# Mixture-of-experts results accumulated in DRAM instead of scattered, read back and added

## The chip, the cores and the metric

The kernel runs on one core of a Trainium2 chip. The metric is the device time of one execution in microseconds (us). All data are float32 unless said otherwise. The core has five engines that run side by side and meet at semaphores: PE (matrix multiply), DVE (vector), ACT (activation functions), POOL (GpSimd, which here also issues the scatters by index), and SP, whose queue issues most plain DMAs.

## The reference, cut to what matters

The whole program is four residual blocks on 4096 tokens of 128 features: a causal convolution with softmax weights, a feed-forward block with FP4-quantized operands, an attention block with two inner training steps, and a mixture of experts. Only the last one matters here:

```python
probs = softmax(layernorm(x) @ Wg + bg)                 # E = 8 experts
gate_vals, exp_idx = top_k(probs, 2)                    # K = 2 experts for a token
gate_vals = gate_vals / sum(gate_vals)
capacity = ceil(1.2 * T * K / E)                        # T = 4096 tokens: 1229 slots an expert
# every expert takes up to 1229 tokens, the rest of its slots stay empty
h  = gelu(buf[e] @ W1[e] + b1[e])                       # 1229 x 128 -> 1229 x 512
ye = h @ W2[e] + b2[e]                                  # 1229 x 512 -> 1229 x 128
out[token] = sum over its two experts of gate * ye[slot of the token]
x = x + out
```

## The kernel before

The tokens live in SBUF as `cx.x`, 128 partitions x 32 tiles x 128 features, in eight groups of four tiles (`G = 4`, `W = 512` columns). Three tables in DRAM belong to the experts (class `Slots`): `rows`, 9856 rows of 130 numbers (a token's normalized features, its result row and its weight; expert e owns `PITCH` = 1232 rows); `res`, 8192 rows of 128 for results, one for each token and choice; and `last`, 4096 rows for the last expert's results, one for each token. `clear` (L1117) fills `rows` with empty entries and `res` and `last` with zeros, by three DMAs on SP's queue, at the end of the first block.

Routing (`route`, from L1198) is called once for each group during the last part of the third block. Each call computes the layernorm, the two experts, the weights and the slots of 512 tokens, and POOL issues eight scatters of 128 rows into `rows` (L1278). The addition that finishes a group's `x` is L876 on DVE.

`experts` (from L1297) then loops over the eight experts. SP loads an expert's slots into `xe` (L1333 for nine full tiles of 128 slots, L1337 for the last 77), two buffers; the loads wait for all routing scatters. A piece is four tiles (512 columns), so an expert is pieces of 4, 4 and 2 tiles. For each piece PE transposes the tiles (`tp`, L1356), DVE copies them (`xt`, L1358), PE multiplies by W1 into four banks `ph` (L1362), ACT applies GELU (`ht`, L1365), PE multiplies by W2 (`po`, L1371), DVE adds the bias (`ye`, L1380) and multiplies by the weight (L1384), and POOL scatters each tile's 128 rows to DRAM (L1386). `ye` has four buffers. Empty slots carry a row number past the table's end, and a bounds check drops them:

```python
1386  sc = nc.gpsimd.indirect_dma_start(
1387      out=(self.slots.last if last else self.slots.res)[:, :],
1388      out_offset=bass.IndirectOffsetOnAxis(ap=num[:m, c0 + i, :], axis=0),
```

For the last expert, DVE first turns the row numbers into token numbers (`tok`, L1345 to L1348). Experts 0 to 6 write to `res`, the last to `last`.

At the end `gather` (L1313) reads `res` back in sixteen DMAs of 256 KB (`y`, L1318, SP's queue, after all scatters to `res`), and DVE adds each to `x` (L1319); then it does the same with `last` in eight DMAs, on SP and ACT. Each finished group goes out by a DMA (L1427, SP's queue).

The order on each engine is fixed at build time from the order of the program and the waits between instructions; an engine executes its list in order. DMAs of one kind share eight semaphores in turn, so a ninth one waits for the first.

Of the kernel before, what the change touches and what calls it, by code (L numbers as in the profile page):

```python
# [8 lines left out]
I32 = mybir.dt.int32  # L9
# [1088 lines left out]
class Slots:  # L1098
# [4 lines left out]
    def __init__(self, cx, stack):  # L1103
        nc, tc = cx.nc, cx.tc
        dram = stack.enter_context(tc.tile_pool(name="d_dram", bufs=1, space=DRAM))
        self.rows = dram.tile([R, DX], F32, tag="rows", name="rows")
        self.res = dram.tile([K * T, D], F32, tag="res", name="res")
        self.last = dram.tile([T, D], F32, tag="last", name="last")
        n = R // P
        m = 7  # L1110
        self.empty = cx.const.tile([P, m, DX], F32, tag="empty", name="empty")
        nc.gpsimd.memset(self.empty, 0.0)
        nc.gpsimd.memset(self.empty[:, :, D : D + 1].bitcast(I32), K * T)
        self.n, self.m = n // m, m

    def clear(self, cx, ins):

        nc = cx.nc
        by_p = self.rows.rearrange("(p a m) d -> p a (m d)", p=P, m=self.m)
        src = flat(self.empty).unsqueeze(1).to_broadcast([P, self.n, self.m * DX])  # L1120
        after(cx.tc, nc.sync.dma_start(out=by_p, in_=src), ins)
        src = cx.const.tile([P, 4 * D], F32, tag="zero", name="zero")
        nc.gpsimd.memset(src, 0.0)
        for t in (self.res, self.last):
            n = t.shape[0] // P // 4
            by_p = t.rearrange("(p a m) d -> p a (m d)", p=P, m=4)
            after(cx.tc, nc.sync.dma_start(out=by_p, in_=src.unsqueeze(1).to_broadcast([P, n, 4 * D])), ins)


class Moe:  # L1130
# [29 lines left out]
    def open_router(self, stack):  # L1160
        cx = self.cx
        nc, tc = cx.nc, cx.tc
        cp = stack.enter_context(tc.tile_pool(name="r_c", bufs=1))
        self.p2 = stack.enter_context(tc.tile_pool(name="r_p2", bufs=2))
        self.ps_t = stack.enter_context(tc.tile_pool(name="r_pst", bufs=1, space=PSUM))
        self.ps_r = stack.enter_context(tc.tile_pool(name="r_psr", bufs=1, space=PSUM))
        tp = self.ps_t.tile([P, E * NF], F32, tag="t", name="tp")
        nc.tensor.transpose(tp, self.b1_rows, cx.ident[: E * NF, : E * NF])
        nc.scalar.copy(self.b1.rearrange("p e c -> p (e c)"), tp)
        self.ones = cp.tile([P, P], F32, tag="ones", name="ones")  # L1170
        nc.gpsimd.memset(self.ones, 1.0)
# [12 lines left out]
        self.rank = cp.tile([P, G, E], F32, tag="rank", name="rank")  # L1184
        nc.gpsimd.iota(
            self.rank, [[0, G], [-1, E]], base=E, channel_multiplier=0, allow_small_or_imprecise_dtypes=True
        )

        self.xr = cp.tile([P, K, NT, DX], F32, tag="xr", name="xr")
        num = cp.tile([P, K, NT], I32, tag="num", name="num")  # L1190
        nc.gpsimd.iota(num, [[T, K], [P, NT]], base=0, channel_multiplier=1)
        nc.gpsimd.tensor_copy(self.xr[:, :, :, D : D + 1].bitcast(I32), num.unsqueeze(3))

        self.seen = cp.tile([P, K, E], F32, tag="seen", name="seen")
        nc.gpsimd.memset(self.seen, 0.0)
        self.limit = nc.gpsimd.to_reg(R - 1)

    def route(self, g):  # L1198
# [8 lines left out]
            return t.unsqueeze(2).to_broadcast([P, G, E])  # L1207

        x, at = grp(cx.x, g), slice(g * G, (g + 1) * G)
        tp = self.ps_t.tile([P, G, P], F32, tag="t", name="tp")  # L1210
        for j in range(G):
            nc.tensor.transpose(tp[:, j, :], x[:, j, :], cx.ident)
# [84 lines left out]
    def experts(self):  # L1297
# [5 lines left out]
        done, ended = [], []  # L1303
        by_t = self.slots.res.rearrange("(k n p) d -> p k n d", k=K, p=P)
        last_t = self.slots.last.rearrange("(n p) d -> p n d", p=P)
        with ExitStack() as st:
            p2 = st.enter_context(tc.tile_pool(name="d_p2", bufs=2))
            ps_t = st.enter_context(tc.tile_pool(name="d_pst", bufs=2, space=PSUM))
            ps_h = st.enter_context(tc.tile_pool(name="d_psh", bufs=4, space=PSUM))
            ps_o = st.enter_context(tc.tile_pool(name="d_pso", bufs=2, space=PSUM))  # L1310
            limit, last_limit = nc.gpsimd.to_reg(K * T - 1), nc.gpsimd.to_reg(T - 1)

            def gather(src, k, names, first, engines):  # L1313

                for g in range(NG):
                    y = p2.tile([P, G, D], F32, tag="y", name="y", bufs=8)
                    eng = engines[g % len(engines)]
                    self.after(eng.dma_start(out=y, in_=src[:, k, g * G : (g + 1) * G, :]), names)  # L1318
                    ad = nc.vector.tensor_tensor(grp(cx.x, g), grp(cx.x, g), y, ALU.add)  # L1319
                    tc.add_manual_dep(  # L1320
                        ad.ins, first.ins.name,
                        mybir.DependencyInfo(mybir.DependencyClass.NoSync, mybir.DependencyReason.DATA),
                        reason="experts first",
                    )

            for e in range(E):
                xe = p2.tile([P, NR, DX], F32, tag="xe", name="xe")
                base = e * PITCH
# [7 lines left out]
                )  # L1336
                self.after(nc.sync.dma_start(out=xe[:left, NR - 1, :], in_=rows[full : base + CAP, :]), every)  # L1337
                num = xe[:, :, D : D + 1].bitcast(I32)
                if last:

                    tok = p2.tile([P, 3, NR], I32, tag="tok", name="tok")
                    for lo, k, m in ((0, NR - 1, P), (NR - 1, 1, left)):
                        t = tok[:m, :, lo : lo + k]
                        n = num[:m, lo : lo + k, 0]
                        nc.vector.tensor_scalar(t[:, 0], n, float(T), None, ALU.is_ge)  # L1345
                        nc.vector.tensor_scalar(t[:, 1], n, float(K * T), None, ALU.is_lt)
                        nc.vector.tensor_tensor(t[:, 0], t[:, 0], t[:, 1], ALU.mult)
                        nc.vector.scalar_tensor_tensor(t[:, 2], t[:, 0], -float(T), n, ALU.mult, ALU.add)  # L1348
                    num = tok[:, 2, :].unsqueeze(2)
                for c0 in range(0, NR, G):  # L1350
                    tiles = range(c0, min(c0 + G, NR))
                    size = [left if i == NR - 1 else P for i in tiles]
                    n = sum(size)
                    tp = ps_t.tile([P, W], F32, tag="t", name="tp")
                    for i, m in zip(tiles, size):
                        nc.tensor.transpose(tp[:, (i - c0) * P : (i - c0) * P + m], xe[:m, i, :D], cx.ident[:m, :m])  # L1356
                    xt = p2.tile([P, W], F32, tag="xt", name="xt")
                    last_in = nc.vector.tensor_copy(xt[:, :n], tp[:, :n])  # L1358
# [17 lines left out]
                    for lo, k, m in ((0, nf, P), (nf, len(size) - nf, left)):  # L1376
# [7 lines left out]
                        last_out = nc.vector.tensor_tensor(y, y, w, ALU.mult)  # L1384
                        for i in range(lo, lo + k):
                            sc = nc.gpsimd.indirect_dma_start(  # L1386
                                out=(self.slots.last if last else self.slots.res)[:, :],
                                out_offset=bass.IndirectOffsetOnAxis(ap=num[:m, c0 + i, :], axis=0),
                                in_=ye[:m, i, :], in_offset=None,
                                bounds_check=last_limit if last else limit, oob_is_err=False,  # L1390
                            )
                            tc.declare_no_dep(sc.ins, group="results", reason="rows of their own")
                            tc.add_to_no_dep_group("results", sc.ins)
                            (ended if last else done).append(sc.ins.name)
            gather(by_t, 0, done, last_in, (nc.sync,))
            gather(by_t, 1, done, last_out, (nc.sync,))
            gather(last_t.unsqueeze(1), 0, ended, last_out, (nc.sync, nc.scalar))


def moe(cx):  # L1400
# [45 lines left out]
```

## Time and profile before

| | |
|---|---|
| Median of three timed runs | 1364.11 us (1363.63 to 1365.26) |
| Profiled execution, its own time | 1367.42 us |
| Its span, first to last instruction | 1365.7 us |
| Mean granted clock of PE | 0.927 |
| Busy: PE, DVE, ACT, POOL | 82%, 57%, 36%, 56% of the span |
| First scatter of results, last one issued | 1180.9 us, 1346.9 us |
| First output DMA issued | 1353.5 us |

The profile is one execution. A row of a group names line, engine and operation, what it writes and reads, the count, the busy time in us and the mean of one in ns, then the idle time of the engine just before such instructions and what ended most of it. "issue" is time in which the engine waited for nothing that the profile shows. A row of the timeline gives start and length in us; a "q" behind an engine's name means its queue, that is DMA issues and waits. The chain of waits lists the work that ended last, in order of time. The PE rows count each of these float32 matrix products as two instructions.

### The profile page before, as it was taken

To read this page: it belongs to the slowest core of one execution; us is meant where nothing else is said; L and a number is where in the kernel's file an instruction comes from. 1 tells how busy PE (TensorE), PEld (TensorE's weight loads), DVE (VectorE), ACT (ScalarE), POOL (GpSimd) and SP (SyncE) were. 2 spreads that over 40 slices of the span, in tenths; PEclk is the share of its full clock that TensorE was granted. 3 is DMA by queue.
4 is the path that set the end of the run, shared out by engine and by line. 5 is a ranking of instruction groups with operands and counts; after the bars stand their busy time and mean duration, and the time that the engine had idled before them with its cause. 6 is when DMAs were issued, how large, how long until landed. Compare 5 with 4: busy or idle time off the path is not lost.

```text
span 1365.7 us, 15325 instructions
## 1 busy us (share of the span) xinstructions
PE 1122.8 (82%) x5211; PEld 661.2 (48%) x5211; DVE 776.2 (57%) x1754; ACT 493.7 (36%) x1002; POOL 761.5 (56%) x724
## 2 busy tenths in 40 slices
PE   4688888726878689999998999999898873799981
PEld 1233333314656445555556455555665442576761
DVE  8689899978796544444445444444556564122233
ACT  4534455325555632222234222222442221333320
POOL 4336566644554588888841888888104336244533
PEclk9888899976999999999999999999999886899996
DMA  4322223924000000000000000000000001222146
GB/s 133 90 73 73 73 73 95 348 82 143 1 0 1 0 0 1 0 0 1 1 1 1 1 0 1 0 1 1 0 1 30 24 28 43 57 60 63 48 114 182
DMA packets 61614, 63.07 MB, mean 46 GB/s; under 512 B 6767, under 2 KB 44478, under 8 KB 61536
## 3 DMA queue, kind: packets, MB, share of 16 engines
q1 hardware_dynamic: 54016, 52.37, 13.1%
q0 software_dynamic: 4608, 8.43, 2.0%
q10 hardware_dynamic: 2912, 1.29, 0.4%
q8 instruction: 41, 0.67, 0.2%
q14 instruction: 37, 0.30, 0.1%
HBM read 37.90 MB, written 25.04 MB: 46 GB/s over the span
## 4 chain that ended last, share of the span: by engine, by line
issue 62%; PE 10%; DMA 2%; DVE 1%; SPq 1%; POOL 1%; POOLq 0%; ACT 0%; another core or an unknown queue 0%; DVEq 0%
PE po L1371 5%; PE ph L1362 5%; DMA w<-in_L_ffn_W 1%; POOL last L1386 1%; DMA y<-last 1%; PE tp L1356 0%; POOLq L1442 0%; DVE ye L1380 0%; DVE xt L1358 0%; DMA xe<-rows 0%; DMA L_ffn_bg<-in_L_ffn_bg 0%; SPq L604 0%; SPq L710 0%; DMA last<-ye,tok 0%; SPq L59 0%
## 5 line engine op out<-in xcount | busy, mean ns | idle before, releaser
L1051 POOL TENSOR_TENSOR ds<-sw,s 128x512 f32<-128x512 f32 x64 | 81.4, 1272 | 86.7 <-DVE sw L1046 86.7
L1278 POOL DMA_INDIRECT rows<-xr,slot x64 | 62.4, 976 | 104.9 <-DVE rs L93 55.6
L1386 POOL DMA_INDIRECT res<-ye,xe x70 | 68.2, 974 | 89.6 <-DVE ye L1384 36.3
L1053 POOL TENSOR_TENSOR ds<-ds,s 128x512 f32<-128x512 f32 x64 | 112.1, 1751 | 5.0
L391 PE MATMUL cv<-pr,sel 128*32 128x512 f32 x512 | 78.4, 691 | 22.5 <-DVE pr L381 22.4
L1044 ACT COPY b<-pb 128x512 f32<-128x512 f32 x64 | 37.4, 585 | 162.1 <-PE pb L1040 161.6
L1365 ACT ACTIVATE ht<-ph,b 128x512 f32<-128x512 f32 (+1 forms) x96 | 55.5, 602 | 107.9 <-PE ph L1362 96.5
L1048 DVE TENSOR_TENSOR h<-sw,b 128x512 f32<-128x512 f32 x64 | 50.2, 784 | 70.6 <-ACT b L1044 70.1
L1371 PEld LDWEIGHTS po<-w,ht 128*128 128x128 f32 (+1 forms) x640 | 79.5, 193 | 15.3 <-issue 9.5
L1052 POOL TENSOR_TENSOR ds<-sw,ds 128x512 f32<-128x512 f32 x64 | 82.5, 1289 | 5.0
L1371 PE MATMUL po<-w,ht 128*128 128x128 f32 (+1 forms) x640 | 83.0, 284 | 2.7 <-ACT ht L1365 2.6
L1054 POOL TENSOR_TENSOR ds<-ds,b 128x512 f32<-128x512 f32 x64 | 81.4, 1271 | 5.0
L1076 PEld LDWEIGHTS pp<-proj,ht 128*128 128x128 f32 x512 | 67.1, 191 | 30.7 <-issue 29.8
L1362 PE MATMUL ph<-xt,w 128*128 128x512 f32 (+1 forms) x192 | 73.9, 522 | 9.6 <-DVE xt L1358 7.6
L383 POOL TENSOR_TENSOR pr<-base,en 128x512 f32<-128x512 f32 x48 | 69.6, 1479 | 21.7 <-ACT en L345 21.7
L381 DVE TENSOR_TENSOR pr<-base,w 128x3072 f32<-128x3072 f32 x24 | 79.6, 3318 | 2.5 <-ACT w L343 2.5
L1380 DVE TENSOR_TENSOR ye<-po,b 128x512 f32<-128x512 f32 (+2 forms) x32 | 14.9, 488 | 112.7 <-PE po L1371 87.1
L1046 DVE TENSOR_TENSOR sw<-pa,s 128x512 f32<-128x512 f32 x64 | 44.2, 691 | 53.6 <-ACT s L1042 53.6
L1071 ACT COPY ht<-pt 128x512 f32<-128x512 f32 x64 | 37.4, 585 | 101.6 <-PE pt L1069 101.6
L1086 PE MATMUL ph<-proj_t,dpt 128*128 128x512 f32 x128 | 71.6, 641 | 0.0
L1088 DVE TENSOR_TENSOR db<-ph,sw 128x512 f32<-128x512 f32 x64 | 44.2, 691 | 47.4 <-PE ph L1086 47.4
L1038 PE MATMUL pa<-gate,kt 128*128 128x512 f32 x128 | 66.8, 604 | 2.5 <-ACT b L1044 2.4
(320 smaller groups left out, 2665.0 us busy)
## 6 DMA issues: line engine op xcount, KB each, us to landing
base<-far SPq DMA_DIRECT2D x64, 268.0 KB
rows<-empty SPq DMA_DIRECT2D x1, 5005.0 KB
xe<-rows SPq DMA_DIRECT2D x8, 585.0 KB
res<-zero SPq DMA_DIRECT2D x1, 4096.0 KB
w<-in_L_ffn_W SPq DMA_DIRECT2D x16, 256.0 KB
y<-res SPq DMA_DIRECT2D x16, 256.0 KB
far<-avg SPq DMA_DIRECT2D x8, 272.0 KB
x<-in_L_attn_x SPq DMA_DIRECT2D x8, 256.0 KB
```

Source lines behind the costliest of these rows:

```text
L381: vec(nc.vector.tensor_tensor(pr[:, :nv, :], s["base"][:, :nv, at], w.to_broadcast([P, nv, L]), ALU.mult))
L383: nc.gpsimd.tensor_tensor(pr[:, d, :], s["base"][:, d, at], s["en"][:, g, :], ALU.mult)
L391: ten(nc.tensor.matmul(s["cv"][32 * j : 32 * (j + 1), :], sel[:, i].rearrange("p a h -> p (a h)"), s["pr"][g][:, i * NJ + j, :], start=(g ...
L1051: nc.gpsimd.tensor_tensor(ds, sw, s, ALU.mult)
L1052: nc.gpsimd.tensor_tensor(ds, sw, ds, ALU.subtract)
L1053: nc.gpsimd.tensor_tensor(ds, ds, s, ALU.add)
L1054: nc.gpsimd.tensor_tensor(ds, ds, b, ALU.mult)
L1076: nc.tensor.matmul(pp, ht[:, c * P : (c + 1) * P], proj[:, c, :], start=(c == 0), stop=(c == NF - 1))
L1086: nc.tensor.matmul(ph, dpt, proj_t, start=True, stop=True)
L1362: nc.tensor.matmul(ph[:, :n], self.w1[:, e, c * P : (c + 1) * P], xt[:, :n], start=True, stop=True)
L1371: nc.tensor.matmul(po[:m, i - c0, :], ht[:, c, at : at + m], self.w2[:, e, c, :], start=(c == 0), stop=(c == NF - 1),)
L1386: sc = nc.gpsimd.indirect_dma_start(out=(self.slots.last if last else self.slots.res)[:, :], out_offset=bass.IndirectOffsetOnAxis(ap=num[: ...
```

## The change

The two result tables go. In their place stands `sums`, 4096 + 1232 rows of 128. While a group is routed, SP copies its finished `x` into `sums`. The experts' scatters add their rows to the token's row in `sums` (an accumulating DMA, issued by POOL). Row numbers are now token numbers for both choices; an empty slot's number is 4096 plus its place in the expert, so that it falls on a row that is not read. DVE computes these numbers in `to`, for each expert. Since a token can belong to two experts, an expert's first scatter waits until the scatters of the expert before have landed: POOL writes a small tile `gate` that waits for them. The last expert's pieces are 4, 2, 2 and 2 tiles. After the last scatters SP writes one row of zeros past the tokens, and the output is copied from `sums` by the eight DMAs, DRAM to DRAM. There is no reading back and no addition on DVE.

```diff
         self.rows = dram.tile([R, DX], F32, tag="rows", name="rows")
-        self.res = dram.tile([K * T, D], F32, tag="res", name="res")
-        self.last = dram.tile([T, D], F32, tag="last", name="last")
+        self.sums = dram.tile([T + PITCH, D], F32, tag="sums", name="sums")
...
-        nc.gpsimd.memset(self.empty[:, :, D : D + 1].bitcast(I32), K * T)
+        nc.gpsimd.memset(self.empty[:, :, D : D + 1].bitcast(I32), T)
...
     def clear(self, cx, ins):
...
-        src = cx.const.tile([P, 4 * D], F32, tag="zero", name="zero")
-        nc.gpsimd.memset(src, 0.0)
-        for t in (self.res, self.last):
-            n = t.shape[0] // P // 4
-            by_p = t.rearrange("(p a m) d -> p a (m d)", p=P, m=4)
-            after(cx.tc, nc.sync.dma_start(out=by_p, in_=src.unsqueeze(1).to_broadcast([P, n, 4 * D])), ins)
...
-        nc.gpsimd.iota(num, [[T, K], [P, NT]], base=0, channel_multiplier=1)
+        nc.gpsimd.iota(num, [[0, K], [P, NT]], base=0, channel_multiplier=1)
...
         x, at = grp(cx.x, g), slice(g * G, (g + 1) * G)
+        nc.sync.dma_start(out=self.slots.sums[:T, :].rearrange("(n p) d -> p n d", p=P)[:, at, :], in_=x)
...
-            def gather(src, k, names, first, engines):
-
-                for g in range(NG):
-                    y = p2.tile([P, G, D], F32, tag="y", name="y", bufs=8)
-                    eng = engines[g % len(engines)]
-                    self.after(eng.dma_start(out=y, in_=src[:, k, g * G : (g + 1) * G, :]), names)
-                    ad = nc.vector.tensor_tensor(grp(cx.x, g), grp(cx.x, g), y, ALU.add)
...
+            place = p2.tile([P, NR], I32, tag="place", name="place", bufs=1)
+            nc.gpsimd.iota(place, [[P, NR]], base=0, channel_multiplier=1)
+            added = []
             for e in range(E):
...
-                if last:
-
-                    tok = p2.tile([P, 3, NR], I32, tag="tok", name="tok")
...
-                for c0 in range(0, NR, G):
-                    tiles = range(c0, min(c0 + G, NR))
+                to = p2.tile([P, NR], I32, tag="to", name="to")
+                for i, k, m in ((0, NR - 1, P), (NR - 1, 1, left)):
+                    t, n = to[:m, i : i + k], num[:m, i : i + k, 0]
+                    nc.vector.scalar_tensor_tensor(t, n, float(T), place[:m, i : i + k], ALU.is_ge, ALU.mult)
+                    nc.vector.tensor_tensor(t, t, n, ALU.add)
+                if added:
+
+                    gate = nc.gpsimd.memset(p2.tile([P, 1], F32, tag="gate", name="gate"), 0.0)
+                    self.after(gate, added)
+                    added = []
+                cuts = list(range(0, NR, G)) if not last else [0, G, G + 2, G + 4]
+                for c0, c1 in zip(cuts, cuts[1:] + [NR]):
+                    tiles = range(c0, c1)
...
                             sc = nc.gpsimd.indirect_dma_start(
-                                out=(self.slots.last if last else self.slots.res)[:, :],
-                                out_offset=bass.IndirectOffsetOnAxis(ap=num[:m, c0 + i, :], axis=0),
-                                in_=ye[:m, i, :], in_offset=None,
-                                bounds_check=last_limit if last else limit, oob_is_err=False,
+                                out=self.slots.sums[:, :],
+                                out_offset=bass.IndirectOffsetOnAxis(ap=to[:m, c0 + i : c0 + i + 1], axis=0),
+                                in_=ye[:m, i, :], in_offset=None, compute_op=ALU.add,
                             )
...
+                            if e:
+                                after(tc, sc, gate, sync=False)
+                            added.append(sc.ins.name)
...
-            gather(by_t, 0, done, last_in, (nc.sync,))
-            gather(by_t, 1, done, last_out, (nc.sync,))
-            gather(last_t.unsqueeze(1), 0, ended, last_out, (nc.sync, nc.scalar))
+            end = nc.sync.dma_start(out=self.slots.sums[T : T + 1, :], in_=self.slots.empty[:1, 0, :D])
+            self.after(end, added)
+        cx.x = self.slots.sums[:T, :].rearrange("(n p) d -> p n d", p=P)
```

More of the change, by code (lines that the diff above doesn't have):

```diff
@@ L1112, in __init__ @@
         nc.gpsimd.memset(self.empty, 0.0)
-        nc.gpsimd.memset(self.empty[:, :, D : D + 1].bitcast(I32), K * T)
+        nc.gpsimd.memset(self.empty[:, :, D : D + 1].bitcast(I32), T)
         self.n, self.m = n // m, m
     def clear(self, cx, ins):
-        nc = cx.nc
         by_p = self.rows.rearrange("(p a m) d -> p a (m d)", p=P, m=self.m)
         src = flat(self.empty).unsqueeze(1).to_broadcast([P, self.n, self.m * DX])
-        after(cx.tc, nc.sync.dma_start(out=by_p, in_=src), ins)
-        src = cx.const.tile([P, 4 * D], F32, tag="zero", name="zero")
-        nc.gpsimd.memset(src, 0.0)
-        for t in (self.res, self.last):
-            n = t.shape[0] // P // 4
-            by_p = t.rearrange("(p a m) d -> p a (m d)", p=P, m=4)
-            after(cx.tc, nc.sync.dma_start(out=by_p, in_=src.unsqueeze(1).to_broadcast([P, n, 4 * D])), ins)
+        after(cx.tc, cx.nc.sync.dma_start(out=by_p, in_=src), ins)
 class Moe:
@@ L1302, in experts @@
         every = [n for s in self.scatters for n in s]
-        done, ended = [], []
-        by_t = self.slots.res.rearrange("(k n p) d -> p k n d", k=K, p=P)
-        last_t = self.slots.last.rearrange("(n p) d -> p n d", p=P)
         with ExitStack() as st:
@@ L1310, in experts @@
             ps_o = st.enter_context(tc.tile_pool(name="d_pso", bufs=2, space=PSUM))
-            limit, last_limit = nc.gpsimd.to_reg(K * T - 1), nc.gpsimd.to_reg(T - 1)
-            def gather(src, k, names, first, engines):
-                for g in range(NG):
-                    y = p2.tile([P, G, D], F32, tag="y", name="y", bufs=8)
-                    eng = engines[g % len(engines)]
-                    self.after(eng.dma_start(out=y, in_=src[:, k, g * G : (g + 1) * G, :]), names)
-                    ad = nc.vector.tensor_tensor(grp(cx.x, g), grp(cx.x, g), y, ALU.add)
[L1320 to L1324, printed above, removed]
+            place = p2.tile([P, NR], I32, tag="place", name="place", bufs=1)
+            nc.gpsimd.iota(place, [[P, NR]], base=0, channel_multiplier=1)
+            added = []
             for e in range(E):
@@ L1338, in experts @@
                 num = xe[:, :, D : D + 1].bitcast(I32)
-                if last:
-                    tok = p2.tile([P, 3, NR], I32, tag="tok", name="tok")
[L1342 to L1349, printed above, removed]
-                for c0 in range(0, NR, G):
-                    tiles = range(c0, min(c0 + G, NR))
+                to = p2.tile([P, NR], I32, tag="to", name="to")
[10 more added lines that the diff above has]
+                    tiles = range(c0, c1)
                     size = [left if i == NR - 1 else P for i in tiles]
@@ L1357, in experts @@
                     xt = p2.tile([P, W], F32, tag="xt", name="xt")
-                    last_in = nc.vector.tensor_copy(xt[:, :n], tp[:, :n])
+                    nc.vector.tensor_copy(xt[:, :n], tp[:, :n])
                     ht = p2.tile([P, NF, W], F32, tag="ht", name="ht")
@@ L1383, in experts @@
                         w = xe[:m, c0 + lo : c0 + lo + k, D + 1].unsqueeze(2).to_broadcast([m, k, D])
-                        last_out = nc.vector.tensor_tensor(y, y, w, ALU.mult)
+                        nc.vector.tensor_tensor(y, y, w, ALU.mult)
                         for i in range(lo, lo + k):
                             sc = nc.gpsimd.indirect_dma_start(
-                                out=(self.slots.last if last else self.slots.res)[:, :],
-                                out_offset=bass.IndirectOffsetOnAxis(ap=num[:m, c0 + i, :], axis=0),
-                                in_=ye[:m, i, :], in_offset=None,
-                                bounds_check=last_limit if last else limit, oob_is_err=False,
+                                out=self.slots.sums[:, :],
+                                out_offset=bass.IndirectOffsetOnAxis(ap=to[:m, c0 + i : c0 + i + 1], axis=0),
+                                in_=ye[:m, i, :], in_offset=None, compute_op=ALU.add,
                             )
-                            tc.declare_no_dep(sc.ins, group="results", reason="rows of their own")
+                            tc.declare_no_dep(sc.ins, group="results", reason="an expert has a token once")
                             tc.add_to_no_dep_group("results", sc.ins)
-                            (ended if last else done).append(sc.ins.name)
-            gather(by_t, 0, done, last_in, (nc.sync,))
-            gather(by_t, 1, done, last_out, (nc.sync,))
-            gather(last_t.unsqueeze(1), 0, ended, last_out, (nc.sync, nc.scalar))
+                            if e:
[4 more added lines that the diff above has]
+        cx.x = self.slots.sums[:T, :].rearrange("(n p) d -> p n d", p=P)
 def moe(cx):
```

## The prediction

> **What bounds the kernel now.** I read the page first, then the chain of waits and the timeline of the last 230 us, then the issues of SP's queue. The change touches three places: the clear (246 us), the experts (1163 to 1338 us) and the tail after them.
>
> The page gives the span and the row of the scatters:
>
> ```profile
> span 1365.7 us, 15325 instructions
> ...
> L1386 POOL DMA_INDIRECT res<-ye,xe x70 | 68.2, 974 | 89.6 <-DVE ye L1384 36.3
> ```
>
> A scatter holds POOL for 974 ns and POOL idles 89.6 us in this row: it waits for results, it does not set the pace. Scatters of 77 and of 128 rows share that mean (966 to 1136 ns over all 70), so most of it does not grow with rows. Back to back they follow at 1.27 us, the extra 0.30 us being "issue".
>
> The end of the chain of waits, in order of time (start, length, what):
>
> ```profile
> 1319.60 5.93 PE po L1371 x26
> 1325.55 0.69 DVE ye L1380
> ...
> 1338.80 5.26 POOLq L1442
> 1344.36 0.97 POOL last L1386
> 1345.63 0.97 POOL last L1386
> 1346.91 2.24 DMA last<-ye,tok
> 1350.85 7.36 DMA y<-last
> ```
>
> From 1325 us on it is not PE. It is POOL's ten scatters of the last expert, one of them stuck for 5.24 us, then the reading back, then the output. The timeline shows the same handover:
>
> ```profile
> 1337.91 0.48 DVE L1384 TENSOR_TENSOR ye<-ye,xe 128x128 f32<-128x128 f32 x2
> ...
> 1346.91 0.97 POOL L1386 DMA_INDIRECT last<-ye,tok  x1 [0.30 <-issue]
> 1349.29 2.01 SPq L1318 DMA_DIRECT2D y<-last  x4
> ...
> 1353.48 7.15 SPq L1427 DMA_DIRECT2D out<-x  x8
> ```
>
> The last result is ready at 1338.39, the last scatter ends on POOL at 1347.88, SP sees it landed at 1349.29 (1.41 us), and 27.3 us lie between the result and the end of the span. So **the tail is serial and short of nothing but order**; before it PE is the bound (46.95 of 50 us busy from 1200 to 1250).
>
> Two more places matter. SP around the clear:
>
> ```profile
> 245.67 0.56 SPq L1121 DMA_DIRECT2D rows<-empty  x1
> 246.27 2.35 SPq L1127 DMA_DIRECT2D res<-zero  x1
> 248.66 14.83 SPq L1127 DMA_DIRECT2D last<-zero  x1
> 295.09 0.34 SPq L605 DMA_DIRECT2D wraw<-in_L_ffn_w_down  x1
> ```
>
> And the handover from an even expert (POOL) to the odd one (DVE):
>
> ```profile
> 1234.51 0.97 POOL L1386 DMA_INDIRECT res<-ye,xe  x1 [0.30 <-issue]
> ...
> 1238.30 0.69 DVE L1380 TENSOR_TENSOR ye<-po,b 128x512 f32<-128x512 f32 x1 [6.50 <-PE po L1371]
> 1238.90 0.68 DVE L1358 COPY xt<-tp 128x512 f32<-128x512 f32 x1
> ```
>
> **What the Trainium skill says.** "DMA: Bandwidth & Descriptors", section "Anatomy of one DMA", puts about 2 us of fixed cost on a DMA, mostly the receipt of the write, heaviest for HBM; the trace agrees (1.41 to 1.78 us from a scatter's end on POOL to the waiting SP issue). Its section "Rules for kernel authors" says that an accumulate reads its destination and writes later, so another must wait for its semaphore: the reason for the gate. Its section "Two DMAs through the same engine are not ordered" reports read-modify-writes that overtake each other, so they are pipelined, not one round trip per row. "Collectives: The Full Stack", section "The bandwidth ceiling: the fold count and why AG ≠ RS ≠ AR", has an adding DMA read two sources and reach half the rate of a copy. No accumulate runs in the kernel before, so no number here confirms the last two.
>
> **The change, part by part.**
>
> 1. *Clear.* Two DMAs of 6 MB go. Nothing waits for them: DMA is idle from 280 us (0.00 busy) and SP's next issue is at 295.09, held by storage. Gain 0. If that cover were gone, 6.3 MB at the 403 GB/s of 260 to 270 us is worth 15.6 us.
>
> 2. *Copy of x to `sums` while routing.* Eight DMAs of 256 KB on SP behind the addition L876; DMA is 10% busy there, a copy takes 1 to 2 us, and POOL's first scatter of the group comes about 8 us after the addition. Behind them SP has only the `xe` loads, which wait for the last routing scatter at 1161.3 anyway. Cost 0; if it did collide with every group's scatters, 8 x 1 us.
>
> 3. *`to`: four small DVE instructions per expert*, about 0.6 us (eight such take 1304.97 - 1303.89 = 1.1 us in `tok`), and a wait: `to` has two buffers, so expert e waits until the scatters of e-2 have landed. DVE executes in order. For e = 2, 4, 6 these stand right before the odd expert's `ye` and `xt`, on which PE waits. POOL's last scatter ends at 1235.48; landed +1.45 = 1236.93, +0.6 = 1237.5, needed at 1238.30: 0.8 us of slack (0.7 at e = 2). For odd e the same place has over 4 us: in the trace `tok` moved such a `ye` from about 1301 to 1305.0 and PE lost nothing. With d the extra landing time of an accumulate and x its extra time on POOL, six scatters standing in the run before it, the cost is 3 x (6x + d - 0.75) where positive.
>    Bounds: d from 0 to 4 us[...]; I take 0.8, since the second read adds only 64 KB, 0.25 us at 267 GB/s, and one more latency. x from 0 to 0.97 (twice the descriptors); I take 0, as the duration does not follow the rows. Neither can be a gain. Cost 3 x 0.05, taken with the nine waits as 0.5 us.
>
> 4. *Gate on POOL.* It waits for the ten scatters before. Behind it on POOL stand only the next expert's scatters, which come after 4.95 to 8.7 us of idle; landing 2.25 us and a memset of some 0.3 us fit. Cost 0; without that cover 2.5 us in each of seven gaps. `xe` loads no longer wait for scatters and come earlier; PE did not wait for them, gain 0.
>
> 5. *Last expert in four pieces of 4, 2, 2, 2 tiles.* In the instruction lists of the two kernels PE's order differs here: `ph` of 512 and 205 columns were interleaved with `po`, the short pieces run one after another. From the end of the first piece at 1325.1: copy ready and first `ph` at 1326.65; `ph` of 256 columns 1.75 us (half of 3.5), wait for GELU 0.9, rest of `po` 1.2, done 1330.5; second 3.85, done 1334.35; transposes, DVE's `ye` and `xt` 1.2; last piece 1.65 + 0.75 + 1.2, done 1339.2, against 1337.47. Cost 1.7 us. DVE done at 1340.2 (before 1338.39).
>
> 6. *Tail.* POOL is no longer behind: two scatters are left. 1340.2 + 0.28 + 0.97 + 0.30 + 0.97 = 1342.7, 5.2 us earlier than 1347.88 (the 5.24 us stall is gone with the 4 MB of `y<-res` that filled the DMAs to 1.15 busy). Landed +1.45 + 0.8 = 1344.95; SP issues a row of zeros, 0.6; then the eight output DMAs, 256 KB each, DRAM to DRAM. Before, reading back and output together moved 4.2 MB from 1349.29 to about 1365.0; less 2 us of latency that is 306 GB/s, and the output alone would take 6.9 us. DRAM at both ends is not in this trace: bounds 306 and 150 GB/s, I take 250, 8.4 us, plus 2.0 us of latency. End 1345.55 + 10.4 + 0.7 = 1356.65, with 0.5 from part 3 1357.2.
>
> **Sum: 1365.7 - 1357.2 = 8.5 us gained.** The profiled execution took 1367.42 us around its span; the three timed runs have a median of 1364.11, 3.3 us less, and I carry the difference over: 1364.1 - 8.5 = 1355.6.
>
> **Rivals.**
> - *Output and landing dear*: 150 GB/s costs 14 us instead of 8.4, gain 2.9 us, 1361. For it: both ends are HBM in pieces of 512 bytes. Against: 317 to 346 GB/s in the last windows, with the same pieces.
> - *A stall goes as well*: PE idled from 1316 to 1319.6 and then ran at clock 0.50 until 1325, behind GELUs that started late for a reason the trace calls "remote". For it: the last expert is rearranged just there. Without it 3.4 us of idle time and about as much of half clock go, 5 to 6 us more, about 1350. Against: ACT's order up to there is unchanged.
> - *Slower: POOL becomes the bound.* Place: the scatters of every expert. Price: an accumulating scatter takes POOL twice as long, 2.24 us at intervals; ten and a gate (2.55) are 25 us an expert against PE's 20.5, so POOL ends near 1180.9 + 200 = 1381, the span near 1395, the time 1393. It decides from about x = 0.45 us on, a scatter of 1.72 us at intervals: parts 3 and 6 together lose 3 x (6x + d - 0.75) + 2x + d = 20x + 4d - 2.25, with d = 0.8, against the 9.8 us that stand without d, x and part 3. For it: two reads per row. Against: 77 rows cost what 128 do.
> - That DRAM is not added to in fact, or the copies remain, is excluded by the compiled instruction lists: no `y`, `res` or `last` is left in them.
>
> **How the numbers follow.** Forecast 0.57 (1352 to 1359), dear output 0.15, stall gone too 0.13, POOL-bound or landing over 3 us 0.12, no change within 0.03. The range 1348 to 1362.5 leaves out the slower cases and the ends. A change of 0.2% is 2.7 us, about what a measurement can tell: faster 0.84, same 0.04, slower 0.12.
>
> **What would show it.** After: scatters `sums<-ye,to` near 974 ns; no `y` rows; DVE's `to` waiting at most about 0.3 us longer than PE allows; last scatter ending on POOL near 1343, first `out<-sums` issue near 1345.5, and about 10 us from there to the end; the stages before 1163 us unchanged. A POOL row above 1.4 us, or PE idle before the odd experts' `ph`, makes it wrong; so does an output longer than 14 us.

## The result, and the profile after

The change made the kernel slower: 1376.17 us (1375.80 to 1378.04) against 1364.68 us for the kernel before beside it, a ratio of 1.0083 with a 95% interval of 1.0064 to 1.0102. The forecast was 1355.6 us. The profiled execution took 1378.04 us, its span 1376.3 us.

The page of the kernel after, its span and the row of the scatters that add (columns: count, then busy time in us and mean ns, then idle time before and what ended most of it):

```profile
span 1376.3 us, 15278 instructions
...
L1365 POOL DMA_INDIRECT sums<-ye,to x80 | 124.8, 1561 | 62.1 <-DVE ye L1363 33.4
```

A scatter that adds holds POOL for 1561 ns where one that overwrites took 974 ns. Back to back they follow at 1.86 us instead of 1.27. This is the 0.58 us that the prediction calls x and took as zero.

The waits of the kernel after (who waits, for whom; us in total, times, longest):

```profile
DVE to L1321 <- DMA sums<-ye,to: 62.6, 6, 12.6
...
PE ph L1341 <- DVE xt L1337: 25.1, 12, 7.5
```

DVE stands 62.6 us in six waits of `to` for scatters to land, and PE stands 25.1 us behind DVE's copies (7.6 us in the kernel before). One such place, where DVE prepares expert 2 in the middle of expert 1; POOL's queue, then DVE's, then PE's timeline of the kernel after (start, length, and in brackets the idle time before):

```profile
1196.49 1.53 POOL L1365 DMA_INDIRECT sums<-ye,to  x1 [0.30 <-issue]
1199.70 0.10 POOL L1325 MEMSET gate<- 128x1 f32 x1 [1.69 <-issue]
1202.38 1.57 POOL L1365 DMA_INDIRECT sums<-ye,to  x1 [2.58 <-DVE xt L1337]
```

```profile
1199.68 0.17 DVE L1321 SCALAR_TENSOR_TENSOR to<-xe,place 128x9 int32<-128x9 int32 x1 [9.70 <-DMA sums<-ye,to]
...
1200.23 0.68 DVE L1359 TENSOR_TENSOR ye<-po,b 128x512 f32<-128x512 f32 x1
1200.83 0.68 DVE L1337 COPY xt<-tp 128x512 f32<-128x512 f32 x1
```

```profile
1201.56 5.40 PE L1341 MATMUL ph<-xt,w 128*128 128x512 f32 x8 [4.61 <-DVE xt L1337]
```

The same products in the kernel before:

```profile
1198.56 3.70 PE L1362 MATMUL ph<-xt,w 128*128 128x512 f32 x8 [0.88 <-DVE xt L1358]
```

Expert 0's last scatter leaves POOL at 1198.02. At 1199.7 two waits for its landing end together: the gate on POOL, and `to` on DVE, whose buffer those scatters were reading. Behind `to` in DVE's order stand `ye` and `xt` of expert 1; so PE waits 4.61 us (0.88 before), and its eight `ph` then take 5.40 us instead of 3.70 (the granted clock is 0.61 from 1201.50 to 1204.00 and 1.00 again from 1207). Before experts 3 and 5 PE waits 7.51 and 7.09 us. POOL in turn waits 2.58 us for that `ye`. It is **a loop**: POOL waits for DVE, DVE for the landing of POOL's scatters. Two experts take 48.2 us on average (the gates at 1199.70 and, six experts later, 1344.31, are 144.6 us apart) where the kernel before took 41.07 (from the `ph` at 1198.56 to those at 1239.64).

The end, in the kernel after's timeline:

```profile
1344.31 0.10 POOL L1325 MEMSET gate<- 128x1 f32 x1 [1.92 <-DMA sums<-ye,to]
...
1351.88 0.48 DVE L1363 TENSOR_TENSOR ye<-ye,xe 128x128 f32<-128x128 f32 x2
...
1361.65 1.52 POOL L1365 DMA_INDIRECT sums<-ye,to  x1 [0.30 <-issue]
1364.90 0.24 SPq L1376 DMA_DIRECT2D sums<-empty  x1
1365.20 6.32 SPq L1408 DMA_DIRECT2D out<-sums  x8
```

The last result is ready at 1352.36 but the last scatter ends at 1363.17: in the last expert POOL works off ten scatters back to back, begun only at 1344.96, after the gate. From there the tail is 13.1 us, shorter than the 17.8 us that the kernel before needed from its last scatter to its end.

### The profile page after: what moved, and what is told of

It is laid out like the page before. It is cut to its first block, busy times and chain, and to the rows that moved or that the text cites. A ratio compares the mean times of both kernels' runs of the same rounds, so it can differ in the third digit from the quotient of the medians.

```text
span 1376.3 us, 15278 instructions
## 1 busy us (share of the span) xinstructions
PE 1124.6 (82%) x5219; PEld 661.5 (48%) x5219; DVE 762.7 (55%) x1757; ACT 494.1 (36%) x1006; POOL 802.3 (58%) x731
## 3 DMA queue, kind: packets, MB, share of 16 engines
q0 software_dynamic: 13440, 9.28, 4.9%
## 5 line engine op out<-in xcount | busy, mean ns | idle before, releaser
L1365 POOL DMA_INDIRECT sums<-ye,to x80 | 124.8, 1561 | 62.1 <-DVE ye L1363 33.4
L1344 ACT ACTIVATE ht<-ph,b 128x512 f32<-128x512 f32 (+2 forms) x100 | 56.0, 588 | 122.1 <-PE ph L1341 121.0
L1341 PE MATMUL ph<-xt,w 128*128 128x512 f32 (+2 forms) x200 | 78.8, 534 | 25.1 <-DVE xt L1337 25.1
L1350 PE MATMUL po<-w,ht 128*128 128x128 f32 (+1 forms) x640 | 80.0, 278 | 0.0
L1076 PE MATMUL pp<-proj,ht 128*128 128x128 f32 x512 | 67.5, 275 | 0.0
```

Source lines behind the costliest of these rows:

```text
L1076: nc.tensor.matmul(pp, ht[:, c * P : (c + 1) * P], proj[:, c, :], start=(c == 0), stop=(c == NF - 1))
L1341: nc.tensor.matmul(ph[:, :n], self.w1[:, e, c * P : (c + 1) * P], xt[:, :n], start=True, stop=True)
L1350: nc.tensor.matmul(po[:m, i - c0, :], ht[:, c, at : at + m], self.w2[:, e, c, :], start=(c == 0), stop=(c == NF - 1),)
L1365: sc = nc.gpsimd.indirect_dma_start(out=self.slots.sums[:, :], out_offset=bass.IndirectOffsetOnAxis(ap=to[:m, c0 + i : c0 + i + 1], axis=0 ...
```

## The experiments

Ratios are to the kernel before on the same chip. Since the profiled executions reach the experts up to 6 us apart (the last routing scatter ends between 1158.1 and 1164.1 us) for no reason in the edits, I also give E, the time **from the end of the last routing scatter to the end of the last result scatter**, read in each timeline: 202.5 us in the kernel after (1160.67 to 1363.17). E comes from one profiled execution of each kernel; e1_to8 and e4_wide, which are alike up to the last scatter, agree within 0.1 us.

**e1_to8: eight buffers of `to`.**

```diff
-                to = p2.tile([P, NR], I32, tag="to", name="to")
+                to = p2.tile([P, NR], I32, tag="to", name="to", bufs=8)
```

> The changed kernel with eight buffers for `to` instead of two, nothing else: DVE's `to` no longer waits until scatters have landed. Theory A (the scatter is 0.58 us longer, and this costs time because DVE stands in order behind POOL: `to` waits for the landing, and `ye` and `xt` wait behind `to`, and PE behind `xt`): the 62.6 us of DVE's waits on `sums<-ye,to` go, PE's 7.5 us stalls before the odd experts go, the last scatter ends on POOL near 1346 us instead of 1363, time 1358 to 1362. Theory B (POOL itself is the bound: ten scatters at 1.86 us, 1.85 us of landing and the gate are 20.7 us against PE's 20.5): the waits move from DVE to POOL's gate, the expert stage shortens by less than 5 us, time above 1371.

Measured: 1362.28 us, ratio 0.9963 (0.9943 to 0.9984), E = 184.6: 0.3 us over theory A's range and far from theory B's. POOL's timeline, the gates alone and the last scatter:

```profile
1243.41 0.10 POOL L1325 MEMSET gate<- 128x1 f32 x1 [1.89 <-DMA sums<-ye,to]
...
1264.14 0.10 POOL L1325 MEMSET gate<- 128x1 f32 x1 [1.77 <-DMA sums<-ye,to]
...
1284.77 0.10 POOL L1325 MEMSET gate<- 128x1 f32 x1 [1.76 <-issue]
...
1346.12 1.52 POOL L1365 DMA_INDIRECT sums<-ye,to  x1 [0.30 <-issue]
```

One word takes away DVE's waits for scatters, PE's stalls before the odd experts' `ph` are back at 0.88 us, and the loop is gone: worth 17.9 us of E. POOL now runs without a gap except at the gates. From gate to gate it takes 20.6 to 20.8 us four times, then 22.6 and 21.4 us for a reason that the trace doesn't name, while PE makes two experts in 40.2 us (its `ph` at 1200.04 and 1240.21), and POOL ends 15.4 us after PE (1347.64 against 1332.24). What is left is the bare POOL bound; e9_two_late puts that to the test.

**e2_plain: scatters that overwrite, `to` with its two buffers** (the addition is left out).

```diff
-                                in_=ye[:m, i, :], in_offset=None, compute_op=ALU.add,
+                                in_=ye[:m, i, :], in_offset=None,
```

> The changed kernel with plain scatters instead of accumulating ones; what is left out is the addition, a token keeps the row that was written last. `to` still has two buffers. Theory A: POOL's scatter is back at 0.97 us, the handovers have their slack again (0.7 to 0.8 us), and the prediction's sum holds apart from this one term: last scatter ends near 1343 us, time 1354 to 1359. Rival C (the wait of `to` for the landing, or the gate, costs by itself, whatever the scatter's length): time stays above 1368.

Measured: 1352.63 us, ratio 0.9907 (0.9875 to 0.9938), E = 179.2. The row of the page and PE at the same place:

```profile
L1365 POOL DMA_INDIRECT sums<-ye,to x80 | 77.2, 965 | 86.8 <-DVE ye L1363 56.4
```

```profile
1196.01 3.70 PE L1341 MATMUL ph<-xt,w 128*128 128x512 f32 x8 [0.87 <-DVE xt L1337]
```

That is 1.4 us under the range I gave, in the direction of theory A. With x gone, the two buffers, the gates, the four `to` instructions and the landing of scatters cost PE nothing at the odd experts. So the two-buffer wait is harmful only together with x: at 965 ns a scatter it does not delay PE, at 1561 ns it closes the loop.

**e3_short: the kernel before with the last expert in pieces of 4, 2, 2 and 2.**

```diff
-                for c0 in range(0, NR, G):
-                    tiles = range(c0, min(c0 + G, NR))
+                cuts = list(range(0, NR, G)) if not last else [0, G, G + 2, G + 4]
+                for c0, c1 in zip(cuts, cuts[1:] + [NR]):
+                    tiles = range(c0, c1)
```

> The kernel before with only the last expert cut into pieces of 4, 2, 2 and 2 tiles. Prediction's parts 5 and 6: PE ends 1.7 us later, POOL starts its fifth scatter about 3 us earlier, but the stall of 5.24 us and the reading back stay; time 1362 to 1366, no difference that counts. Rival: the pieces alone empty POOL's queue before the reading back fills the DMAs and the stall goes: time 1356 to 1360.

Measured: 1368.14 us, ratio 1.0011 (1.0003 to 1.0019). It lies over the range I gave, but so did the kernel before beside it (1366.15). The short pieces alone bring nothing: a scatter is still stuck (4.99 us, before 5.24). POOL's timeline, then DVE's:

```profile
1341.95 4.99 POOL L1387 DMA_INDIRECT last<-ye,tok  x1 [1.22 <-DVE ye L1385]
```

```profile
1341.80 5.02 DVE L1319 TENSOR_TENSOR x<-x,y 128x512 f32<-128x512 f32 x8
```

The stuck scatter lies beside a block of DVE's additions of `y` and ends with it. The kernel before shows the same: its 5.24 us scatter (1338.82 to 1344.06) lies beside DVE's additions from 1338.31 to 1343.21, and three of 1.47 to 1.51 us beside those from 1327.63 to 1332.52. The DMAs were 4% busy there from 1340 to 1345, so reading `res` does not explain that stall. (In e3_short `y<-res` was still being read beside the stuck scatter.) That the additions cause the stall is suggested by the times alone; no run here tests it. The change takes the additions away as well.

**e4_wide: as e1_to8, the output in rows of 2048 bytes** instead of 512 (four tokens that lie together in DRAM).

```diff
+        flat_o = out.rearrange("b l d -> (b l) d").rearrange("(g p n) d -> g p (n d)", p=P, n=G)
+        flat_s = cx.slots.sums[:T, :].rearrange("(g p n) d -> g p (n d)", p=P, n=G)
...
-            nc.sync.dma_start(out=grp(ot, g), in_=grp(cx.x, g))
+            nc.sync.dma_start(out=flat_o[g], in_=flat_s[g])
```

> As e1_to8, and the eight output DMAs read and write 2048 contiguous bytes per row of the access pattern instead of four pieces of 512 bytes. If the output's 11 us (1365.2 to 1376.3) are set by pieces of 512 bytes, it falls to 7 to 9 us and the time is 2 to 4 us under e1_to8; if by bytes through DRAM at both ends or by latency, the same as e1_to8 within 1 us.

Measured: 1361.10 us, ratio 0.9959 (0.9942 to 0.9976), E = 184.7; from the first output issue to the end 10.3 us, in e1_to8 10.5. The size of the pieces does not set the output's time.

**e5_early: as e1_to8, expert 0 cut so that POOL starts earlier.**

```diff
-                cuts = list(range(0, NR, G)) if not last else [0, G, G + 2, G + 4]
+                cuts = {0: [0, 1, 2, 4, 6, 8], E - 1: [0, G, G + 2, G + 4]}.get(e, list(range(0, NR, G)))
```

> The changed kernel with eight buffers of `to`, and expert 0 cut into pieces of 1, 1, 2, 2, 2 and 2 tiles (before: 4, 4, 2). Theory A (with the buffers mended, POOL's queue alone sets the end: 80 scatters at 1.86 us and seven gates, back to back from the first scatter on): POOL's first scatter comes 4 to 6 us earlier than 1179.7, all gates and the last scatter (1347.6 in e1_to8) come earlier by the same amount, and the time is 1357 to 1359 against 1362.3, though PE does more small instructions. Rival: PE or the weights' waits bound the first expert, the scatters come with gaps in expert 0, and at most 1 us is gained.

Measured: 1359.62 us, ratio 0.9963 (0.9947 to 0.9978), E = 186.1. A miss, and the trace shows where: the first scatter came 12.2 us after routing instead of 18.9, but POOL's timeline now has gaps:

```profile
1176.99 1.55 POOL L1365 DMA_INDIRECT sums<-ye,to  x1 [2.33 <-DVE ye L1363]
...
1194.61 0.10 POOL L1325 MEMSET gate<- 128x1 f32 x1 [1.83 <-DMA sums<-ye,to]
1197.97 1.57 POOL L1365 DMA_INDIRECT sums<-ye,to  x1 [3.27 <-DVE xt L1337]
```

PE makes an expert in about 20.1 us and POOL needs 20.7 or more, so work that POOL begins earlier isn't there to continue with: expert 1's first piece of four tiles is ready even later (38.7 us after the last routing scatter, in e1_to8 37.6). "Back to back from the first scatter on" was wrong of me; it is back to back from the second piece of expert 1 on.

**e6_long: as e1_to8, last expert in 4, 4, 2 again.**

```diff
-                cuts = list(range(0, NR, G)) if not last else [0, G, G + 2, G + 4]
+                cuts = list(range(0, NR, G)) if not last else [0, G, 2 * G]
```

> The changed kernel with eight buffers of `to`, and the last expert in pieces of 4, 4 and 2 tiles again (instead of 4, 2, 2, 2). Theory A (POOL is 14 us behind PE at the end, so it does not matter how early the last results are there): within 1 us of e1_to8 (1362.3), last scatter of POOL at the same time within 0.5 us. Rival (short pieces are needed for the end of the change): 2 us or more slower than e1_to8.

Measured: 1360.21 us, ratio 0.9955 (0.9939 to 0.9972), E = 185.8. The median is 2.1 us under e1_to8's, more than the 1 us I allowed, but on another chip; the ratio is that of e1_to8 (0.9963) well within both intervals, and E is 1.2 us longer. No difference is shown: while POOL is behind, how the last expert is cut matters little.

**e7_half: as e1_to8, each scatter adds 64 rows.**

```diff
-                                out_offset=bass.IndirectOffsetOnAxis(ap=to[:m, c0 + i : c0 + i + 1], axis=0),
-                                in_=ye[:m, i, :], in_offset=None, compute_op=ALU.add,
+                                out_offset=bass.IndirectOffsetOnAxis(ap=to[:64, c0 + i : c0 + i + 1], axis=0),
+                                in_=ye[:64, i, :], in_offset=None, compute_op=ALU.add,
```

> The changed kernel with eight buffers of `to`; each scatter adds only its first 64 rows (the other rows of each tile are left out). Theory A (the 0.58 us that an accumulating scatter takes on POOL over a plain one is a fixed addition): the row of the scatters stays at 1.5 us or more, and the intervals near 1.8 us. Rival (POOL pays for each row's descriptors, twice as many for an accumulate): about 1.25 us or less, and POOL stops being the bound: time near 1353.

Measured: one run, 1352.66 us, E = 175.8. The time is the rival's, and PE sets the pace again (three spans of two gates take 40.1 to 40.5 us). For the row neither theory's number came: it lies between. The page's row, and the line of the DMA queue that carries all scatters (packets, MB, share), which in the kernel after reads 13440 packets and in e2_plain 4608:

```profile
L1365 POOL DMA_INDIRECT sums<-ye,to x80 | 113.1, 1413 | 47.8 <-DVE ye L1363 24.6
```

```profile
q0 software_dynamic: 8448, 6.87, 3.6%
```

In e2_plain 144 scatters make 4608 packets, 32 each. Taking 32 for each of the 64 routing scatters leaves (13440 - 2048) / 80 = 142.4 packets on average for a scatter that adds (72 have 128 rows, eight have 77), and (8448 - 2048) / 80 = 80 for one of 64 rows. So 62.4 packets fewer save 0.148 us, 2.4 ns each. By that price the 110 packets that a full adding scatter has over a plain one (965 ns) account for 0.26 us of the 0.60 us; the other 0.33 us stay unexplained by packets. **By this estimate x is about half a fixed addition and about half a price per packet.** It is a line through two points of one execution each, carried on down to 32 packets, where no adding scatter was run; and packets and rows fell together, so it does not show which of them POOL pays for.

**e8_two and e9_two_late: two tables of sums, so that a gate waits for older scatters.** (Both also copy x to the second table.)

```diff
-                if added:
+                if added[e % 2]:
...
-                    self.after(gate, added)
-                    added = []
+                    self.after(gate, added[e % 2])
+                    added[e % 2] = []
...
-                                out=self.slots.sums[:, :],
+                                out=(self.slots.sumb if e % 2 else self.slots.sums)[:, :],
```

> The changed kernel with eight buffers of `to`, and two tables of sums: even experts add to one, odd ones to the other, so an expert's gate waits for the scatters of the expert before the last, which have long landed. The second table is not added to the output (its results are left out); eight more copies of x go out while routing. Theory A (POOL's queue is the bound and each gate adds about 2.1 us to it): the gates wait 0.3 us or less, POOL needs 18.6 us of 20.5 for an expert, PE sets the pace again, the last scatter ends near 1337 to 1339 and the time is 1351 to 1355 against 1362.3 of e1_to8. Rival (the gates stand in time that POOL has anyway): 1360 or more.

Measured: 1353.27 us, ratio 0.9901 (0.9876 to 0.9927), E = 182.9. The time is as expected and the reason is not. POOL's timeline:

```profile
1199.38 1.53 POOL L1367 DMA_INDIRECT sums<-ye,to  x1 [0.30 <-issue]
1202.57 0.10 POOL L1327 MEMSET gate<- 128x1 f32 x1 [1.66 <-issue]
1203.39 1.57 POOL L1367 DMA_INDIRECT sumb<-ye,to  x1 [0.73 <-issue]
```

Expert 2's gate stands ahead of expert 1's scatters, since nothing ordered it after them, and so it waits for scatters just issued, as before. The time came from the output: it was copied from the even experts' table, whose last scatter is an expert earlier, and began at 1330.09, beside expert 7. This run says nothing of what the gate costs. e9_two_late orders the gate after the last scatter `sc` of the expert before, and takes the output from the table that expert 7 adds to:

```diff
+                    after(tc, gate, sc, sync=False)
...
-                                out=(self.slots.sumb if e % 2 else self.slots.sums)[:, :],
+                                out=(self.slots.sums if e % 2 else self.slots.sumb)[:, :],
```

> As e8_two (two tables of sums, eight buffers of `to`, the table of the even experts left out of the output), with two mends: each gate stands on POOL's queue after the scatters of the expert before, where e8_two had it one expert too early, so that it waited for scatters just issued; and the output is copied from the table of the odd experts, so that it cannot start before the last ones. Theory A (a gate costs POOL's queue about 2.1 us an expert, and POOL's queue is the bound): gates wait 0.3 us or less, PE sets the pace again, and from the last routing scatter to the end of the last result scatter it takes 177 to 180 us (184.6 in e1_to8, 179.2 in e2_plain); time about 5 us below e1_to8, 1355 to 1358. Rival (gates stand in time that POOL has anyway): 184 us and 1360 or more.

Measured: 1349.24 us, ratio 0.9897 (0.9868 to 0.9926), E = 177.2:

```profile
1214.52 1.53 POOL L1368 DMA_INDIRECT sums<-ye,to  x1 [0.31 <-issue]
1215.48 0.68 POOL L1327 MEMSET gate<- 128x1 f32 x1
1217.97 1.57 POOL L1368 DMA_INDIRECT sumb<-ye,to  x1 [1.80 <-DVE ye L1366]
```

The gate no longer waits, and POOL again waits for DVE's results: 7.4 us less E than e1_to8, at nearly the same length of a scatter (1555 ns, there 1561). PE sets the pace, with two experts in 40.2 us. So where POOL is the bound, a gate is not free; and with both waits out of the way the longer scatter is hidden behind PE. The time, under the range of 1355 to 1358, fell by more than E: the profiled execution also reached the experts early, at 1158.44 (1163.02 in e1_to8), so 13 us below e1_to8 is not all the gates' doing.

**e10_mid: as e6_long, expert 0 in pieces of 2, 2, 4 and 2.**

```diff
-                cuts = list(range(0, NR, G)) if not last else [0, G, 2 * G]
+                cuts = [0, 2, G, 2 * G] if not e else list(range(0, NR, G))
```

> As e6_long (eight buffers of `to`, last expert in pieces of 4, 4, 2), and expert 0 in pieces of 2, 2, 4 and 2. Theory A (POOL's queue from the first scatter on; e5_early lost its early start again because six small pieces held PE up): first scatter 3 us earlier, the end 2 to 3 us earlier than e6_long, 1357 to 1358.5. Rival (what the start gains PE gives back before expert 1's first result, as in e5_early): within 1 us of e6_long, 1359.5 to 1361.

Measured: 1359.68 us, ratio 0.9970 (0.9959 to 0.9982), E = 186.3: the rival holds. The start was 4.4 us earlier, and POOL then waited 5.42 us at once for the piece of four.

**e11_both: a whole version.** As e9_two_late, with x copied to the even table alone and the odd one cleared, and a sum at the end:

```diff
+            for g in range(NG):
+                self.after(nc.sync.dma_start(out=grp(cx.x, g), in_=even[:, g * G : (g + 1) * G, :]), added[0])
+            for g in range(NG):
+                y = p2.tile([P, G, D], F32, tag="y", name="y", bufs=8)
+                eng = (nc.sync, nc.scalar)[g % 2]
+                self.after(eng.dma_start(out=y, in_=odd[:, g * G : (g + 1) * G, :]), added[1])
+                ad = nc.vector.tensor_tensor(grp(cx.x, g), grp(cx.x, g), y, ALU.add)
+                after(tc, ad, last_out, sync=False)
```

> A whole version out of e9_two_late: even experts add to one table, which gets x while routing, odd ones to another, which is cleared with zeros at the end of the first block (2 MB, as the kernel before cleared its tables). After expert 6 has landed SP reads the even table into the tokens' tiles, beside expert 7; after the last scatters the odd table is read back on SP and ACT, DVE adds the two, and the groups go out from SBUF as in the kernel before. Theory A (gates off POOL's path are worth 7 us, reading back beside the end costs about 5 us: the kernel before took 15.7 us from its first y<-last to the end of the output, e9_two_late 10.7): last scatter as in e9_two_late, 177 to 178 us after the last routing scatter, time 1353 to 1356, faster than e1_to8 (1362.3) and before by 0.7 to 0.9%. Rival (reading the even table beside expert 7's scatters fills the DMAs and holds up those scatters, or the tail is dearer): 1358 or more.

Measured: 1356.62 us, ratio 0.9940 (0.9926 to 0.9953), E = 176.8. SP's timeline:

```profile
1320.00 6.98 SPq L1386 DMA_DIRECT2D x<-sumb  x8
1338.93 2.01 SPq L1390 DMA_DIRECT2D y<-sums  x4
1343.04 7.22 SPq L1422 DMA_DIRECT2D out<-x  x8
```

The even table is read beside expert 7 and hardly holds up a scatter (two of the ten take 1.67 and 1.72 us, the others 1.52 to 1.58). From the first `y<-sums` to the end of the span it takes 16.0 us. It is 0.6 us over the range I gave and faster than the kernel before. That it is faster than e1_to8 too is likely but not shown: the ratio there is 0.9963, and the two intervals overlap (0.9926 to 0.9953 and 0.9943 to 0.9984).

## Why the prediction was wrong

**Steps 1 and 2, the clear and the copies of x: right, 0.** In the kernel after SP issues `rows<-empty` at 244.53 and nothing until 294.06, as before; the last routing scatter starts at 1159.70 (before 1160.36), and PE's work up to 1163 us is equal (964.8 us busy in both). A copy of x took 2.3 us from issue to landing, where I had 1 to 2.

**Step 3, `to`: here it failed**, in the words "I take 0, as the duration does not follow the rows". The observation was true of scatters that overwrite: the trace has them at 32 packets each. It says nothing of one that adds, which has 142 packets on average. x is 0.587 us (1561 less 974 ns), inside the bounds of 0 to 0.97 that I gave, but I chose the lower bound. That alone would have turned the sign: at x = 0.587 and with my d of 0.8 my own sum loses 20 x 0.587 + 3.2 - 2.25 = 12.7 us against the 9.8 us gained elsewhere. (With the d of 0.3 that was measured, below, it loses 10.7, so the sum alone gives only about 1 us of the 11.5 by which the kernel became slower; the rest is in the terms that follow.)

Two more terms of this step were too small. I let six scatters stand in the run before the landing; it was ten in every even expert. In expert 0 four scatters at 1.86 us outlast the gap to the second piece's results (1.40 us before, against 4x = 2.35), and from its first scatter to its last it takes 18.35 us instead of 13.55. In expert 2 the run takes 18.57 us instead of 14.90, and it starts 2.2 us later behind PE, because the odd experts' `to` blocks DVE as well: "for odd e the same place has over 4 us" did not survive x, DVE waited 9.33 us until 1225.33. And a stall of PE costs more than its wait: after the three stalls the eight `ph` take 5.40, 5.23 and 5.14 us instead of 3.70, 1.56 us more on average. By the measured terms 10 x 0.587 + 0.3 - 0.75 + 1.56 = 7.0 us for two experts, where the gates show 48.2 - 41.07 = 7.1. My formula gave 6 x 0.587 + 0.8 - 0.75 = 3.6. Its other term, d, was smaller than the 0.8 I took: from the end of POOL's last scatter to the gate it is 1.68 to 2.10 us in the kernel after, and 1.37 to 1.71 us at six of e2_plain's seven gates (the seventh, 3.26, stands by itself), so about 0.3 us.

**Step 4, the gate: cost 0 was right only with its cover.** I named POOL's idle 4.95 to 8.7 us as what hides it. With x the cover is gone: 7.4 us lie in the gates once `to` is mended (e1_to8 against e9_two_late). The price that I named without the cover, 2.5 us in each of seven gaps, is near the 2.0 to 2.2 us by which five of e1_to8's seven gates hold up POOL's queue, but only about 1.1 us a gate shows in E, since PE needs its 20.1 us an expert anyway.

**Step 5, short pieces: small either way.** e3_short's ratio of 1.0011 is 1.5 us, where I had a cost of 1.7; e6_long is like e1_to8. They only help if POOL keeps up, and it did not.

**Step 6, the tail: the start of it wrong, its length right.** "POOL is no longer behind" failed with x: its last scatter ended at 1363.17 instead of 1342.7. From there I had put 13.95 us and it took 13.1: the landing 1.73 us (I had 2.25), SP's row 0.30 (0.6), the output 11.1 us (10.4 + 0.7). The 5.24 us stall of a scatter did go, but my reason for it, that `y<-res` filled the DMAs, does not fit the trace (see e3_short).

As a check of the whole: e2_plain is the change with x = 0. From the first to the end of the last scatter it takes 160.3 us, forecast 161.8 (1342.7 less 1180.9); by its ratio it gains 12.7 us, forecast 8.5. That the first two agree so well is partly luck: PE's stall before the last expert went, which I had left as a rival, and in the last expert DVE waited 4.59 us (until 1328.29) for scatters to land, which no step priced, and PE 2.42 us behind it.

**The rivals.** "POOL becomes the bound" is what happened. It was to decide from x = 0.45 on, and x came out at 0.587. Its own price took a scatter twice as long and found 1393; the pure POOL bound at the true x is e1_to8's 1362, and the other 14 us came from the loop through DVE. The rival's threshold had that loop in it, through step 3's formula; its price did not. "Output dear" is refuted (11.1 us). "A stall goes as well" came true, since PE no longer idles before the last expert (its `po` of 26 products take 3.18 us, 5.93 before), but could not show in the kernel after, since POOL ended last. Why the GELUs were late in the kernel before, and in e3_short, but not in any kernel with `sums`, stays open: no run separates it.

**The skill against the runs.** "DMA: Bandwidth & Descriptors", section "Anatomy of one DMA", puts the fixed cost of a DMA at about 2 us, mostly the receipt; the 1.68 to 2.10 us at the gates agree. Its table there calls descriptor generation "small, variable"; the runs differ, as a scatter that adds holds POOL 0.59 us longer and then lands only some 0.3 us later. "Perfetto Trace Analysis", section "DMA Instruction — SWDGE (GPSIMD)", says that the profiler's end of such an instruction is the end of generating descriptors, not of moving data. That agrees with e7_half, where a scatter with fewer packets holds POOL for less time, and it would have told me to look for more descriptors on POOL first. The halved rate of an adding DMA, which the prediction drew on, no run here separates from the rest of the 0.3 us.

## What to carry to other kernels

When an edit changes the kind of an instruction, an old row's insensitivity to size is no price for the new kind; put the upper bound through the plan and see whether the sign holds, above all if the issuing engine has to do ten of them for each step of the bound. A small index tile that a DMA reads needs enough buffers that its writer does not wait for the DMAs that read it, or that engine will stand there with all its later work behind it; here one word, `bufs=8`, was worth 17.9 us of E and 13.9 us between the medians. And a wait that is free because its engine idles must be priced again whenever that engine gets more to do.

## What was not expected of the hardware

- An indirect scatter of rows of 512 bytes that adds takes POOL 1561 ns against 965 to 974 ns for one that overwrites, with 142 against 32 packets (means over 72 scatters of 128 rows and eight of 77); with 64 rows it takes 1413 ns and 80 packets.
- From its end on POOL to its landing takes only about 0.3 us more than for one that overwrites (1.68 to 2.10 against 1.37 to 1.71 us, one of 3.26 us left aside).
- Scatters that overwrite took 1.47 to 5.24 us on POOL, instead of 0.97, beside blocks of DVE's additions of `y` (four in the kernel before); that the one causes the other is not shown.
- A copy of 2 MB from DRAM to DRAM ran at 267 and 298 GB/s in two windows of 3 us in the kernel after, in pieces of 512 bytes, and at 268 and 300 GB/s in pieces of 2048 bytes in e4_wide, with less of the DMAs' time busy (share 0.77 to 0.80 against 0.96 to 1.01).
